# One layer of the second image pair is issued beside the first pair's later layers

## The chip, the cores and the metric

The kernel runs on one core of one Trainium2 chip. The metric is the device time of one execution in microseconds (us). Its engines are named as in the profile: PE (TensorE, matmuls), DVE (VectorE), ACT (ScalarE), POOL (GpSimd) and SP (SyncE, which here only issues DMAs). "Granted clock" is the share of its full speed that TensorE's clock was given in a stretch.

## What is computed

A batch of 8 images of 64 channels and 64 x 64 pixels goes through four layers in turn, all in float32:

```python
# layer 0: full self-attention over the 4096 pixels of an image (bn + relu values), then
#          a depthwise 3x3 conv, a 1x1 conv and a residual
# layer 1: two blocks of 8x8 window attention (the second shifted) with an MLP each
# layer 2: a 3x3 filter made of a spatial and a channel part, then a 1x9 conv and a residual
# layer 3: selective scan over 4 directions with 16 states, then a small multi-scale stage
def step(h, inp):
    u_t, dt_t, B_t, C_t = inp
    h = h * jnp.exp(dt_t[..., None] * A) + dt_t[..., None] * B_t[:, :, None, :] * u_t[..., None]
    return (h, jnp.einsum('bkcn,bkn->bkc', h, C_t))
x = _L0_conv_ref(x, ...)
x = _L1_conv_ref(x, ...)
x = _L2_conv_ref(x, ...)
x = _L3_conv_ref(x, ...)
```

Pixels are only mixed within an image, so different images are independent of each other.

## The kernel before

Two images form a pair: their 2 x 64 channels fill the 128 partitions, and a pair's activation `X` is one 128 x 4096 slab (2 MB). There are four pairs, p = 0 to 3. For each pair there are three kinds of work:

- **front(p)** (L1230): `layer0`, `layer1`, `layer2` and `scan_sources`. It is a Python generator which issues a few instructions and then yields a number, its own estimate of their cost. By these numbers `layer0` costs 702 units, `layer1` 784, `layer2` 286 and `scan_sources` 245, 2016 in all.
- **scans(p)** (L1619): 64 units (2 images x 4 directions x 8 pieces of 512 pixels) of 8 steps each, so 512 steps. A step takes two of the 16 states: `fetch` brings two rows each of B and C from memory, spread over all partitions (L1682), `products` multiplies on POOL (L1687), `step` makes two exponentials on ACT (L1707) and two scans on DVE (L1710), multiplies by C on POOL or, in part, on DVE (L1721 to L1724), and `sums` adds both states up on PE (L1737).
- **back(p)** (L1755): what follows the scan, costed as a quarter of a front.

The order: front(0) runs alone. Then scans(0) runs with front(1) beside it, scans(1) with back(0) and front(2), scans(2) with back(1) and front(3), scans(3) with back(2), and back(3) runs alone. "Beside" is done in the issuing order: after step i of the 512, `scans` draws from the other generators until they have issued the share (i + 1) / (512 - 24) of their total cost. So a step carries 2016 / 488 = 4.13 units of front(1) in scans(0), and the last 24 steps carry none. A scheduler then orders instructions by priority (the order of issue) and readiness.

In `layer0` the main loop runs over 8 column pieces and 32 row tiles: two score matmuls `s` (L1271, one per image), two exponentials `e` (L1277), two value matmuls `po` (L1263), 2.2 units each time. In `layer1`, `window_head` (L1342) and `window_row` (L1383) work on rows of 8 windows: scores `w_s` (L1398), exponentials `w_e` (L1415), values `w_av` (L1425), 37 units a row, 16 rows; `mlp` (L1479) follows twice. `layer2`'s inner loop has nine pairs of a `pb` (L1532) and an `acc` matmul (L1536) per chunk, and `py` (L1546).

Buffers: PSUM is cut into two pools. `ps` holds three rotating banks "da" and one bank "y" (sum of a scan), `pf` three rotating banks "f" and one "acc". The scans draw from `ps`, a front from `pf`. When `turn` is not negative, `bank` (L1179) hands out "f" and "da" in turn, so a front that runs alone has six rotating banks; this is set for front(0). In SBUF there are three slabs in one pool, the scans' buffers (`Y`, 16 KB a partition, and the pool `scan`) stand below them, and each stage opens a small pool of its own (`w0`, `w0b`, `w1n` and so on).

Of the kernel before, what the change touches and what calls it, by code (L numbers as in the profile page):

```python
# [1 line left out]

# [1 line left out]

# [5 lines left out]
F32 = mybir.dt.float32  # L10
# [7 lines left out]
P = 128  # L18
# [6 lines left out]
TD = 512  # L25
NTD = L // TD
LEAD = 24
TC = 1024
NTC = L // TC
SLAB = 66 * 66  # L30
# [195 lines left out]
class _Net:  # L226
    def __init__(self, ctx, tc, x, packs, layout, out):
        self.tc, self.nc = tc, tc.nc
        self.x, self.out = x, out
        nc = self.nc  # L230
        self.const = ctx.enter_context(tc.tile_pool(name="const", bufs=1))
        self.dram = ctx.enter_context(tc.tile_pool(name="rows", bufs=2, space=bass.MemoryType.DRAM))
        self.packs, self.layout, self.w = packs, layout, {}
        self.load(self.const, (0, 1))
        with tc.tile_pool(name="temp", bufs=1) as temp:
            self.load(temp, (2,))
            self.prepare()
# [910 lines left out]
class _Direct:  # L1148
# [8 lines left out]
    def __init__(self, net, ctx):  # L1157
        self.net, self.tc, self.nc, self.w = net, net.tc, net.nc, net.w
        tc = self.tc
        self.dram = ctx.enter_context(tc.tile_pool(name="mem", bufs=2, space=bass.MemoryType.DRAM))  # L1160
        one = ctx.enter_context(tc.tile_pool(name="scan1", bufs=1))
        self.Y = one.tile([P, L], F32, name="Y", tag="Y")
        self.carries = one.tile([P, NST], F32, name="carry", tag="carry")
        self.sw = ctx.enter_context(tc.tile_pool(name="scan", bufs=2))
        self.slabs = ctx.enter_context(tc.tile_pool(name="slabs", bufs=3))
        self.ps = ctx.enter_context(tc.tile_pool(name="ps_scan", bufs=3, space=PSUM))
        self.pf = ctx.enter_context(tc.tile_pool(name="ps_front", bufs=3, space=PSUM))
        self.kept = {}
        self.turn = -1

    def padded(self, name):
        t = self.slabs.tile([P, SLAB], F32, name=name, tag="slab").rearrange("p (h w) -> p h w", w=66)
# [6 lines left out]
    def bank(self, name, shape=(P, CH), ours="f"):  # L1179

        if self.turn >= 0:
            self.turn += 1
            ours = ("f", "da")[self.turn % 2]
        return (self.pf if ours == "f" else self.ps).tile(list(shape), F32, name=name, tag=ours)

    def total(self, name, shape=(P, CH)):
        return self.pf.tile(list(shape), F32, name=name, tag="acc", bufs=1)
# [40 lines left out]


    def front(self, p):  # L1230
        X = yield from self.layer0(p)
        yield from self.layer1(X)
        yield from self.layer2(X)
        yield from self.scan_sources(p, X)

    def layer0(self, p):


        nc, tc, w, net, half = self.nc, self.tc, self.w, self.net, self.HALF
        X = self.flat("X")  # L1240
        nc.sync.dma_start(X, self.net.x[2 * p : 2 * p + 2].rearrange("b c h w -> (b c) (h w)"))
        att = self.padded("att")
        VT = self.flat("VT").rearrange("p (t c) -> p t c", c=P)

        def at(rows, t):
            return X[rows, t * P : (t + 1) * P]

        with tc.tile_pool(name="w0", bufs=2) as wk:
            for g in range(8):
                pv = self.bank("pval", (P, 4, P))  # L1250
                nc.tensor.matmul(pv, lhsT=net.ones[0:1, :], rhs=net.b1row.rearrange("o a c -> o (a c)").unsqueeze(1).to_broadcast([1, 4, P]), start=True, stop=False)
                for j in range(4):
                    nc.tensor.matmul(pv[:, j, :], lhsT=at(slice(0, P), 4 * g + j), rhs=net.w1bd, start=False, stop=(j == 3))
                nc.scalar.activation(VT[:, 4 * g : 4 * g + 4, :], pv, AF.Relu)
                yield 4

            parts = wk.tile([P, 2, 32, NCH], F32, name="parts", tag="parts", bufs=1)
            for jc in range(NCH):
                po = self.total("po")

                def weigh(t, es):
                    for im in range(2):
                        nc.tensor.matmul(  # L1263
                            po[half[im]], lhsT=VT[:, t, half[im]], rhs=es[im], start=(t == 0), stop=(t == 31)
                        )

                last = None
                for t in range(32):
                    ss = [self.bank(f"s{im}") for im in range(2)]
                    for im in range(2):  # L1270
                        nc.tensor.matmul(  # L1271
                            ss[im], lhsT=at(half[im], t), rhs=X[half[im], jc * CH : (jc + 1) * CH], start=True, stop=True
                        )
                    es = []
                    for im in range(2):
                        e = wk.tile([P, CH], F32, name="e", tag="e", bufs=6)
                        nc.scalar.activation(  # L1277
                            e, ss[im], AF.Exp, scale=C**-0.5, accum_out=parts[:, im, t, jc : jc + 1]
                        )
                        es.append(e)  # L1280
                    if last is not None:
                        weigh(*last)
                    last = (t, es)
                    yield 2.2
                weigh(*last)
                nc.vector.tensor_copy(self.rows(att, jc), self.img(po))

            sums = net.sums[:, p]
            nc.vector.tensor_reduce(sums, parts, AX.X, ALU.add)
            rec = wk.tile([P, 2, 32], F32, name="rec", tag="rec", bufs=1)  # L1290
            nc.vector.reciprocal(rec, sums)
            for g in range(8):
                pr = self.bank("prec")
                for j in range(4):
                    for im in range(2):
                        nc.tensor.matmul(
                            pr[half[im], j * P : (j + 1) * P],
                            lhsT=rec[:, im, 4 * g + j : 4 * g + j + 1].to_broadcast([P, 64]),
                            rhs=w["ident"],
                            start=True,  # L1300
                            stop=True,
                        )
                d = self.rows(att, g)
                nc.vector.tensor_tensor(d, d, self.img(pr), ALU.mult)
                yield 4
        with tc.tile_pool(name="w0b", bufs=2) as wk:
            for c in range(NCH):
                acc = self.bank("cacc", (P, 8, 64))
                yield from self.dwconv(acc, att, 8 * c, 8, w["dw2"], None)
                cv = wk.tile([P, 8, 64], F32, name="cv", tag="cv")  # L1310
                nc.scalar.activation(cv, acc, AF.Relu, scale=net.bn23[:, 0:1], bias=net.bn23[:, 1:2])
                pw = self.bank("pw")
                nc.tensor.matmul(pw, lhsT=w["w3bd"], rhs=cv, start=True, stop=True)
                t = wk.tile([P, CH], F32, name="t", tag="t")
                nc.scalar.activation(t, pw, AF.Identity, scale=net.bn23[:, 2:3], bias=net.bn23[:, 3:4])
                x = X[:, c * CH : (c + 1) * CH]
                nc.vector.tensor_tensor(x, x, t, ALU.add)
                yield 3
        return X
# [514 lines left out]
            net.log_exp(last)  # L1834


@with_exitstack
def tile_kernel(ctx: ExitStack, tc: tile.TileContext, x: bass.AP, packs, layout, out: bass.AP):
    net = _Net(ctx, tc, x, packs, layout, out)
    with ExitStack() as path:  # L1840
        net.open(path, True)
        d = _Direct(net, path)
        net.log_exp()
        d.turn = 0
        front = d.run(d.front(0))
        d.turn = -1
        back = 0.25 * front
        for p in range(B // 2):
            works, cost = [], 0
            if p:  # L1850
                works.append(d.back(p - 1))
                cost += back
            if p + 1 < B // 2:
                works.append(d.front(p + 1))
                cost += front
            d.scans(p, d.chain(*works), cost)
        d.run(d.back(B // 2 - 1))

    with tc.tile_pool(name="check", bufs=1) as pool:
        bad = net.in_range(pool)  # L1860
    with tc.If(bad > 0), ExitStack() as path:
        net.open(path, False)
        for p in range(B // 2):
            t = net.layer0(p)
            t = net.layer1(t)
            t = net.layer2(t)
            net.layer3(t, p)
# [21 lines left out]
```

## Time and profile before

| | us |
|---|---|
| median of 3 runs (14009.71 to 14023.95) | 14022.91 |
| the profiled execution | 14012.53 |
| its span, first to last instruction | 14010.7 |
| front(0) alone, until the first product of scans(0) | about 1880 |
| scans(0) with front(1), first to last sum | 1904 to 4915 |
| scans(1) with back(0), front(2) | 4934 to 8257 |
| scans(2) with back(1), front(3) | 8277 to 11611 |
| scans(3) with back(2) | 11632 to 13760 |
| back(3) alone | 13760 to 14010 |

The page's line of 40 slices shows the same in coarse: POOL has nothing to do in the first five slices, which are front(0). Busy shares over the whole span are 81% for PE, 60% for DVE, 50% for ACT and 58% for POOL. They are averages over these stages and say little of any one of them. In scans(3), which has little beside it, POOL is busy for 1819.91 of 2128 us, and a step takes 4.2 us.

The page follows the chain of waits backward from the last instruction over the last stage alone; for the stages that the change touches it has no entry, and the tables by stage are used instead.

### The profile page before, as it was taken

The page shows a single profiled execution, that of the slowest core. Times are in us where ns is not written, and L with a number is a line of the kernel's source. Part 1 is how long each engine was busy: PE and PEld are TensorE (multiplying, and loading weights), DVE is VectorE, ACT ScalarE, POOL GpSimd, SP SyncE. Part 2 cuts the span into 40 slices and gives each one's busy share as a digit, 9 for nine tenths or more (in the row PEclk, how much of TensorE's full clock was granted, in tenths as well). Part 3 has the DMA queues.
Part 4 walks back from the last instruction along what each step waited for, and adds up shares of the span by engine and source line. Part 5 has one row for each costly group of instructions (what it writes and reads, how often), then busy time and mean ns, then how long its engine had stood idle before and what let it go on. Part 6 is the DMA issues. An engine that isn't in the chain of part 4 may idle for free. (4 is left out here: it accounts for less than half of the span.)

```text
span 14010.7 us, 141613 instructions
## 1 busy us (share of the span) xinstructions
PE 11364.2 (81%) x46358; PEld 4240.7 (30%) x46358; DVE 8425.0 (60%) x9763; ACT 7041.2 (50%) x15460; POOL 8178.9 (58%) x4111
## 2 busy tenths in 40 slices
PE   9888979978888669988889667997998866666665
PEld 2255222234433222224433222223443222222221
DVE  0222254477766874356675767337666677997875
ACT  5533156556544645555553645555554554454442
POOL 0000046578767765556665685457666688878982
PEclk9966789989889789998899788998888878888887
DMA  0000044456555754445554675335544577878882
GB/s 17 1 1 2 6 163 162 159 185 226 195 181 189 246 195 149 135 154 176 176 177 160 227 248 172 131 132 189 173 163 166 183 253 259 273 250 275 276 273 97
DMA packets 705499, 2379.23 MB, mean 170 GB/s; under 512 B 81060, under 2 KB 81188, under 8 KB 703980
## 3 DMA queue, kind: packets, MB, share of 16 engines
q1 hardware_dynamic: 681024, 2315.57, 48.9%
q10 hardware_dynamic: 23724, 54.50, 1.0%
q8 instruction: 367, 6.01, 0.2%
q14 instruction: 384, 3.15, 0.1%
HBM read 2269.08 MB, written 100.66 MB: 169 GB/s over the span
## 5 line engine op out<-in xcount | busy, mean ns | idle before, releaser
L1687 POOL TENSOR_TENSOR vd<-B,du 128x1024 f32<-128x1024 f32 x2048 | 4841.8, 2369 | 3920.1 <-DMA B<-rows 2103.0
L1737 PE MATMUL yd<-vd,pack 128*128 128x512 f32 x8192 | 4625.9, 695 | 1265.4 <-POOL vd L1721 449.5
L1710 DVE TENSOR_TENSOR_SCAN hd<-dad,carry,vd 128x512 f32<-128x512 f32 x2464 | 3093.2, 1271 | 1146.2 <-ACT dad L1707 669.9
L1707 ACT ACTIVATE dad<-du,As 128x512 f32<-128x512 f32 x4096 | 2718.4, 680 | 1017.3 <-DVE hd L1710 701.9
L1737 PEld LDWEIGHTS yd<-vd,pack 128*128 128x128 f32 x8192 | 1624.1, 215 | 3956.6 <-issue 1863.1
L1721 POOL TENSOR_TENSOR vd<-hd,C 128x1024 f32<-128x1024 f32 x768 | 1811.7, 2359 | 1324.0 <-DVE hd L1710 695.7
L1723 POOL TENSOR_TENSOR vd<-hd,C 128x512 f32<-128x512 f32 x1280 | 1637.0, 1280 | 317.9 <-DVE hd L1710 230.0
L1277 ACT ACTIVATE e<-s 128x512 f32<-128x512 f32 x2048 | 1199.2, 591 | 1030.1 <-PE s L1271 1028.6
L1710 DVE TENSOR_TENSOR_SCAN dad<-dad,carry,vd 128x512 f32<-128x512 f32 x1120 | 1427.6, 1275 | 126.5 <-POOL vd L1687 77.5
L1271 PE MATMUL s<-X 64*128 64x512 f32 x4096 | 1343.5, 647 | 105.5 <-ACT e L1277 105.3
L1263 PE MATMUL po<-e,VT 128*64 128x512 f32 x4096 | 1155.4, 631 | 19.0 <-ACT e L1277 19.0
L1718 ACT ACTIVATE carry<-hd 128x1 f32<-128x1 f32 (+1 forms) x1792 | 357.3, 201 | 1225.9 <-DVE hd L1710 1215.5
L1724 DVE TENSOR_TENSOR vd<-dad,C 128x512 f32<-128x512 f32 x1280 | 860.9, 673 | 72.7 <-ACT carry L1718 62.4
L1425 PEld LDWEIGHTS w_av<-vals,w_e 64*64 64x64 f32 x16384 | 630.9, 163 | 204.5 <-ACT w_e L1415 99.4
L1425 PE MATMUL w_av<-vals,w_e 64*64 64x9 f32 x16384 | 658.6, 218 | 38.2 <-ACT w_e L1415 38.0
L1271 PEld LDWEIGHTS s<-X 64*128 64x128 f32 x4096 | 363.5, 187 | 1052.4 <-issue 823.7
L1710 DVE TENSOR_TENSOR_SCAN hd<-dad,vd 128x512 f32<-128x512 f32 x352 | 420.1, 1211 | 191.7 <-ACT dad L1707 88.3
L1748 DVE TENSOR_TENSOR Y<-Y,yd 128x512 f32<-128x512 f32 x128 | 124.8, 975 | 661.3 <-PE yd L1737 661.1
L1718 ACT ACTIVATE carry<-dad 128x1 f32<-128x1 f32 x1120 | 189.5, 169 | 616.6 <-DVE dad L1710 614.4
L1415 ACT ACTIVATE w_e<-w_e 128x512 f32<-128x512 f32 x512 | 310.8, 627 | 360.7 <-DVE w_e L1410 239.4
L1410 DVE TENSOR_TENSOR w_e<-w_s,bias 128x512 f32<-128x512 f32 x512 | 328.8, 682 | 236.3 <-PE w_s L1398 235.3
L1263 PEld LDWEIGHTS po<-e,VT 128*64 128x64 f32 x4096 | 212.9, 136 | 824.6 <-issue 581.0
(247 smaller groups left out, 11150.5 us busy)
## 6 DMA issues: line engine op xcount, KB each, us to landing
B<-rows SPq DMA_DIRECT2D x2048, 512.0 KB, 5.0
C<-rows SPq DMA_DIRECT2D x2048, 512.0 KB, 4.5
xs<-xt SPq DMA_DIRECT2D x128, 256.0 KB, 2.9
xs<-xc SPq DMA_DIRECT2D x128, 256.0 KB, 3.4
xc<-xcv ACTq DMA_DIRECT2D x64, 256.0 KB, 3.8
zs<-z ACTq DMA_DIRECT2D x64, 256.0 KB, 3.8
xt<-XT ACTq DMA_DIRECT2D x32, 512.0 KB, 7.8
rows<-bc SPq DMA_DIRECT2D x256, 64.0 KB, 2.0
```

The lines of the kernel that those rows point to most:

```text
L1263: nc.tensor.matmul(po[half[im]], lhsT=VT[:, t, half[im]], rhs=es[im], start=(t == 0), stop=(t == 31))
L1271: nc.tensor.matmul(ss[im], lhsT=at(half[im], t), rhs=X[half[im], jc * CH : (jc + 1) * CH], start=True, stop=True)
L1277: nc.scalar.activation(e, ss[im], AF.Exp, scale=C**-0.5, accum_out=parts[:, im, t, jc : jc + 1])
L1425: nc.tensor.matmul(self.av[half[im], x % 4 + j, h, :], lhsT=es[h // 4][half[im], j, h % 4, :], rhs=V[half[im], x + j, h, :], start=True, s ...
L1687: self.nc.gpsimd.tensor_tensor(v, st["B"], dx.to_broadcast([P, 2, TD]), ALU.mult)
L1707: nc.scalar.activation(da, u["du"][:, 0], AF.Exp, scale=net.As[:, k, n : n + 1])
L1710: nc.vector.tensor_tensor_scan(along(to), along(da), along(v[:, j]), first, ALU.mult, ALU.add)
L1718: nc.scalar.activation(cs, ends, AF.Copy)
L1721: st["w"] = nc.gpsimd.tensor_tensor(v, h, CC, ALU.mult)
L1723: st["w"] = nc.gpsimd.tensor_tensor(v[:, 0], h[:, 0], CC[:, 0], ALU.mult)
L1724: nc.vector.tensor_tensor(v[:, 1], hs[1], CC[:, 1], ALU.mult)
L1737: m = nc.tensor.matmul(y, lhsT=w["ident"], rhs=st["v"][:, j], start=(n == 0), stop=(n == NST - 1))
```

## The change

`layer0` of pair 1 is taken out of scans(0). It is issued in a new method `begin`, beside `layer1`, `layer2` and `scan_sources` of pair 0, in that order of issue: after `layer0` of pair 0 is done (front now yields a 0 there), it draws 0.8 units of the other generator for each unit of front(0). With 702 units to issue it is through after 702 / 0.8 = 877 units of front(0), that is after all of `layer1` (784) and the first 93 units of `layer2`. Its three slabs and one working pool lie where `Y` and the scans' pool are opened afterwards. Its result goes to memory (2 MB) and front(1) starts by loading it, in the place of the load of the input. Its PSUM is the pool `ps`, three banks "da" and the bank "y". `turn` stays negative in front(0), which therefore has the three banks "f" instead of six, in its own `layer0` too. In scans(0), the cost beside is 1315 units instead of 2016.

```diff
+AHEAD = 0.8
...
+    def begin(self, ctx):
...
+        with tc.tile_pool(name="slabs0", bufs=3) as slabs, tc.tile_pool(name="w00", bufs=2) as pool:
+            ahead = _Apart(self, slabs, pool).first(1)
+            front = first = done = 0
+            for cost in self.front(0):
+                front += cost
+                if cost == 0:
+                    first = front
+                while first and done < AHEAD * (front - first):
+                    done += next(ahead, front)
+            self.run(ahead)
+        one = ctx.enter_context(tc.tile_pool(name="scan1", bufs=1))
+        self.Y = one.tile([P, L], F32, name="Y", tag="Y")
+        self.carries = one.tile([P, NST], F32, name="carry", tag="carry")
+        self.sw = ctx.enter_context(tc.tile_pool(name="scan", bufs=2))
+        return front, first
...
     def front(self, p):
-        X = yield from self.layer0(p)
+        if ("first", p) in self.kept:
+            X = self.flat("X")
+            self.nc.sync.dma_start(X, self.kept["first", p])
+        else:
+            X = yield from self.layer0(p)
+        yield 0
...
+class _Apart(_Direct):
...
+    def bank(self, name, shape=(P, CH)):
+        return self.ps.tile(list(shape), F32, name=name, tag="da")
+
+    def total(self, name, shape=(P, CH)):
+        return self.ps.tile(list(shape), F32, name=name, tag="y", bufs=1)
...
+    def first(self, p):
+        X = yield from self.layer0(p)
+        kept = self.kept["first", p] = self.memory("first")
+        self.nc.sync.dma_start(kept, X)
...
-        d.turn = 0
-        front = d.run(d.front(0))
-        d.turn = -1
+        front, first = d.begin(path)
...
-                cost += front
+                cost += front if p else front - first
```

More of the change, by code (lines that the diff above doesn't have):

```diff
@@ L1 @@
-from contextlib import ExitStack
+from contextlib import ExitStack, nullcontext
 import numpy as np
@@ L1160, in __init__ @@
         self.dram = ctx.enter_context(tc.tile_pool(name="mem", bufs=2, space=bass.MemoryType.DRAM))
[L1161 to L1164, printed above, removed]
         self.slabs = ctx.enter_context(tc.tile_pool(name="slabs", bufs=3))
@@ L1169, in __init__, with work @@
         self.turn = -1
+    def begin(self, ctx):
+        tc = self.tc
+        with tc.tile_pool(name="slabs0", bufs=3) as slabs, tc.tile_pool(name="w00", bufs=2) as pool:
[13 more added lines that the diff above has]
+        return front, first
+    def work(self, name):
+        return self.tc.tile_pool(name=name, bufs=2)
     def padded(self, name):
@@ L1246, in at @@
             return X[rows, t * P : (t + 1) * P]
-        with tc.tile_pool(name="w0", bufs=2) as wk:
+        with self.work("w0") as wk:
             for g in range(8):
@@ L1305, in layer0 @@
                 yield 4
-        with tc.tile_pool(name="w0b", bufs=2) as wk:
+        with self.work("w0b") as wk:
             for c in range(NCH):
@@ L1834, in back, with __init__, work @@
             net.log_exp(last)
+class _Apart(_Direct):
+    def __init__(self, d, slabs, pool):
+        self.net, self.tc, self.nc, self.w = d.net, d.tc, d.nc, d.w
+        self.ps, self.slabs, self.pool, self.dram, self.kept = d.ps, slabs, pool, d.dram, d.kept
+    def bank(self, name, shape=(P, CH)):
+        return self.ps.tile(list(shape), F32, name=name, tag="da")
+    def total(self, name, shape=(P, CH)):
+        return self.ps.tile(list(shape), F32, name=name, tag="y", bufs=1)
+    def work(self, name):
+        return nullcontext(self.pool)
+    def first(self, p):
+        X = yield from self.layer0(p)
+        kept = self.kept["first", p] = self.memory("first")
+        self.nc.sync.dma_start(kept, X)
 @with_exitstack
```

## The prediction

> **What bounds the kernel now.** I read the line of slices first, then cut the span at the stages' borders (first and last sum of each scan, first and last matmul of each layer) and asked for the busy table of these stretches, then for the PE's timeline inside them, and last for who waited for whom. The table of stretches (us; per engine busy time and count; granted clock; DMA share; GB/s):
>
> ```profile
> 62.00:592.00 530.00, 530.00 (x2028) 129.54 (x2024) 4.85 (x7) 320.41 (x1016) 0.00 (x0) 1.00 0.00 1
> 648.00:1502.00 854.00, 717.05 (x6392) 395.35 (x6390) 225.70 (x447) 311.17 (x465) 0.00 (x0) 0.66 0.01 2
> 1904.00:2872.00 968.00, 928.25 (x2698) 257.42 (x2698) 429.64 (x404) 565.21 (x1591) 595.55 (x290) 0.98 0.49 165
> 3090.00:3448.00 358.00, 329.74 (x3282) 172.73 (x3281) 263.85 (x341) 204.22 (x407) 277.21 (x136) 0.91 0.64 213
> 4068.00:4527.00 459.00, 418.12 (x833) 152.20 (x832) 292.53 (x336) 174.99 (x371) 298.93 (x147) 0.92 0.52 175
> 1904.00:4915.00 3011.00, 2606.91 (x11328) 972.14 (x11326) 1940.84 (x2182) 1672.44 (x3698) 2096.44 (x1018) 0.91 0.57 192
> 8215.00:8252.00 37.00, 21.28 (x35) 7.49 (x36) 26.61 (x26) 12.68 (x22) 37.00 (x19) 0.87 0.72 254
> ```
>
> Line 1 is the main loop of layer0 for pair 0: PE without a gap at full clock, 530 us for 256 tiles, 2.07 us a tile. Line 2 is front(0) from the end of layer0 to 93 units into layer2, exactly what the change puts beside the other layer0: PE looks 84% busy, but at a clock of 0.66, the other engines are mostly idle. Lines 3 to 5 are scans(0) beside layer0, the first window attention and layer2 of pair 1; PE is busy for 96, 92 and 91%. Line 6 is scans(0) whole. Line 7 shows scan steps with nothing beside them: POOL has no gap, at two steps in 8.27 us on its timeline, 4.14 us a step. What a busy PE is worth at either clock is seen in two timelines, of layer2 alone (clock 0.50 there) and of window attention inside scans(0):
>
> ```profile
> 1419.23 2.07 PE L1532 MATMUL pb<-f,pack 18*128 18x512 f32 x2
> 1421.23 2.08 PE L1536 MATMUL acc<-tap,pack 128*128 128x512 f32 x2
> ...
> 3130.78 1.02 PE L1662 MATMUL pdd<-xs,xdt 128*128 128x512 f32 x2
> 3131.63 1.02 PE L1359 MATMUL w_q<-w_h,pack 128*128 128x512 f32 x2
> 3189.96 1.98 PE L1737 MATMUL yd<-vd,pack 128*128 128x512 f32 x4
> 3195.37 2.04 PE L1425 MATMUL w_av<-vals,w_e 64*64 64x9 f32 x64
> ```
>
> A float32 matmul of 512 columns is two records: 2.0 us a pair at half clock, about 0.96 from start to start at full clock. That POOL, in scans(0), waits for the PE more than for anything else is in the waits of POOL over 1904 to 4915:
>
> ```profile
> POOL vd L1687 <- PE yd L1737: 303.2, 107, 12.5
> POOL vd L1721 <- issue: 182.6, 40, 9.7
> POOL vd L1721 <- DVE hd L1710: 180.5, 63, 10.4
> ```
>
> **What the skill says.** "TensorE: Matmul & The Clock Gate", What's actually happening: the matrix clock stands at half unless recent activity releases it, and only the two shares 4/8 and 8/8 occur. This trace agrees: the stretches' 0.66 is a mean of 0.50 and 1.00, and the pairs above take 2.0 against 0.96 us. "Perfetto Trace Analysis", Identifying the Most-Contended Engine: matmul busy time is a bad measure of the distance to the engine's limit. Here line 2 says so: 84% busy, at two thirds of the clock. "PSUM — Partial Sum Buffer", Specifications: eight banks a partition, which is why the second stream needs the scans' four, and front(0) loses three.
>
> **The change, part by part.** I count PE work as full-clock demand, from start-to-start times at clock 1.00.
>
> 1. Layer0 of one pair: main loop 530 us; eight `pval` groups at about 2 us, 16; `prec` 8 and eight `pw` 8. Sum 562 us. The convolution's DVE work (72 operations of 0.74 us, 54 us in all) can lie beside PE.
>
> 2. What stands in 648 to 1502: a window row is 4 x 1.02 (`w_s`, 16 records) + 4 x 1.97 (`w_av`, 64 records) + 1.1 + 0.96 + 0.93 + 0.95 (`pc`, `pv`, `w_q`, `w_k`) + 1.08 (`w_vv`) + 0.9 (`w_ot`) + 1.0 (`w_pp`) = 18.9 us; 16 rows 302. First norm 8 x 1.82 = 15. Two MLPs, 16 x 3.9 = 62. Layer2 chunks at 2 x 0.96 + 9 x 2.0 + 7.9 = 27.8, 2.45 of them (85 units of 34.7 after the eight copies): 68. Sum 447 us, which took 854: half of the stretch is a slow clock and waits.
>
> 3. Together 1009 us of demand. PE doesn't run at 100% of demand where streams are mixed. Scans(0) and scans(1) show how far it gets: a step's own demand is 1.91 (`yd`) + 1.94 / 8 (`pdd`, `pbc`) = 2.15 us. Beside layer0: 256 tiles in 143 steps, 1.79 x 2.07 + 2.15 = 5.86 against 6.76 us measured, 87%. Beside window attention (0.51 us a unit): 296 units in 68 steps, 4.37 against 5.27, 83%; in scans(1) 296 in 47.5, 5.33 against 6.81, 78%. Beside layer2: 0.78 a unit, 5.1 against 6.12, 84%. I take 84%, since dense layer0 tiles are 56% of the mix: 1009 / 0.84 = 1201 us. Against 854 the opening grows by **+347**. Bounds: 92% gives 1097 (+243), 74% gives 1363 (+509).
>
> ACT would be busy 311 + 256 x 1.58 (exponential and its accumulator read, two each) + 20 = 735 of 1201 us and DVE under 300: neither becomes the bound. Behind a waiting PE or ACT instruction the other stream's work is queued too: a row's `window_head` makes PE wait for square, logarithm, exponential and a DVE product. PE's waits in 650 to 1500 sum to about 140 us, the longest kinds being:
>
> ```profile
> PE w_q L1359 <- DVE w_h L1355: 36.9, 16, 2.3
> PE ph L1490 <- DVE m_h L1486: 36.2, 16, 2.5
> ```
>
> Layer0's tiles are independent of these and fill part; the rest is in the 84%.
>
> 4. Scans(0) loses layer0: 1315 units over 488 steps, 2.69 a step instead of 4.13. PE demand falls to 2.15 + about 0.6 x 2.69 = 3.8 us a step, which at 83% is 4.6; POOL needs 2096 / 512 = 4.1; DVE (1941 less some 80 of layer0's: its convolution, copies and adds) / 512 = 3.6. So three engines come near each other, and what is late next is POOL, then the chain through DVE. By stage: window attention cost 5.27 us a step at 4.35 units and 6.81 at 6.23, 0.82 us a unit, so the line would pass under POOL's floor; I take 4.7 for 220 steps. Layer2: 6.12 at 3.81 and 7.37 at 5.02, so 5.0 at 2.69; 4.9 for 106 steps. The MLP took 5.3 us at both densities, so something other than PE holds it; 5.0 for 71 steps with the norm. Sources 5.8 and 6.4; 4.9 for 91. Sum 1033 + 519 + 355 + 446 = 2353, and 24 steps without company at 4.15 add 100: 2453 against 3011, **-558**. Bounds: 4.4 a step (2247, -764) and 5.2 (2638, -373).
>
> 5. Small parts. Three banks instead of six for layer0 of pair 0: the same loop has three inside scans(0), and its tiles start 2.06 us apart there (2200.86, 2202.92), so I price it at +10 for the handovers and layer2's rest, bounds 0 and +50. The load of `X` for front(1) was there before (one SP DMA, issued at 1862.56) and is as large; the store of 2 MB is issued on SP at about two thirds of front(0), where DMA is 1% busy, with only the stores of `x2` behind it. At the 190 to 290 GB/s seen in scans it takes some 7 to 11 us, hidden; uncovered it would cost those 11. The input's load for pair 1 has its own slab and lands during layer0 of pair 0. The scans' buffers wait for slabs that are free 300 us earlier.
>
> Sum: 347 - 558 + 10 = **-201**. On the profiled execution 14012.5 gives 13,812; the median of the runs shown stands 10 above it, so 13,822 us.
>
> **Rivals.** (a) *Larger gain*: layer0 keeps the clock at 1.00 and fills every gap, 92%, and scans(0) gets to 4.4 us a step: 243 - 764 + 10 = -511, 13,512. For it: beside layer0 the clock is 0.98. Against: no mixed stretch exceeds 87%, and a POOL-bound 4.4 occurs only where PE is little used.
> (b) *Conserved*: PE sets both stretches and work is just moved; 80% gives +407, scans(0) at 5.1 gives -422: -5, 14,018. For it: the MLP's 5.3. Against: POOL's waits for PE vanish and half the opening's clock is unused.
> (c) *Slower*: the gate doesn't open. Window attention's 64-row tiles leave the clock at 0.66 when alone; if interleaved layer0 runs at that too, its 562 us take 851 beside the 717 already busy, 1568: +714. With -558 and +10 that is +166, 14,189. It decides from the point where the joint stretch is longer than 1402 us (72% of demand). For it: 78% was seen in scans(1). Against: clock 0.91 in attention beside `yd`, whose share of the demand was lower (49%) than layer0's here.
> That the streams don't overlap at all would be 854 + 562 / 0.97, +579, nearly (b).
>
> **Numbers.** Chances: forecast 0.62, (a) 0.13, (b) 0.10, (c) 0.15. A measurement of this kernel tells about 0.2% (28 us) from nothing. Faster: 0.62 + 0.13 + a little of (b), 0.77; within 0.2%: most of (b), 0.08; slower 0.15. Range: the forecast's bounds combined (not both ends at once) reach from about -380 to +10; (a) and (c) leave their outer halves out: 13,640 to 14,050.
>
> **What would show it.** Right: the joint stretch from 648 lasts near 1200 us with PE over 90% busy and a clock above 0.85; first sum of scans(0) near 2260; its sums span near 2450 us at about 4.8 us a step, with POOL's wait for `yd` well under 303 us. Wrong: a clock under 0.75 in the joint stretch (c), or steps above 5.2 us with little on PE, which would mean that a chain or the rows' DMA, not PE, sets scans(0). Scans(1) to (3) should keep 3323, 3334 and 2128 us.

## The result: 13791 us, and where the time went

| | before | changed |
|---|---|---|
| median, us (4 runs each) | 14016.31 | 13791.44 |
| lowest to highest | 13987.48 to 14023.95 | 13790.06 to 13842.86 |
| ratio, 95% interval | | 0.9847, 0.9828 to 0.9867 |

The changed kernel is 225 us faster by the medians. The profiled execution took 13842.86 us, the longest of its four, so the two profiles differ by 170 us only; the stages below are those of the profiles. First the table of stretches of the changed kernel (us; per engine busy time and count; granted clock; DMA share; GB/s):

```profile
62.00:600.00 538.00, 538.00 (x2033) 132.24 (x2032) 4.85 (x7) 322.52 (x1017) 0.00 (x0) 1.00 0.00 1
648.00:1840.00 1192.00, 1162.67 (x8581) 453.61 (x8580) 320.31 (x586) 637.70 (x1486) 0.00 (x0) 0.94 0.01 4
1840.00:2190.00 350.00, 246.56 (x374) 77.94 (x372) 145.06 (x222) 84.78 (x121) 0.00 (x0) 0.68 0.10 37
2222.00:4720.00 2498.00, 2004.36 (x9112) 811.69 (x9110) 1860.46 (x2078) 1372.21 (x2664) 2092.46 (x1021) 0.88 0.68 232
2257.00:2821.00 564.00, 467.34 (x3514) 215.75 (x3512) 415.48 (x479) 298.99 (x614) 485.81 (x238) 0.90 0.67 231
```

Line 1 is the main loop of layer0 for pair 0, as before. Line 2 is the joint stretch, from 648 until layer0 of pair 1 is done: 1192 us where 854 stood, PE busy for 98% at a clock of 0.94. (It reaches a little further into layer2: 57 of its 144 `acc` records have begun at 1840, against 42 at 1502 before. Further down, stretches are compared at the same record.) Line 3 is what is left of front(0), at the old 0.68. The first sum of scans(0) comes at 2222 instead of 1904, so the opening grew by 318 us. Line 4 is scans(0): 2498 us against 3011, 513 less. Line 5 is its first window attention, 118 steps at 4.78 us. The rest of the kernel holds 3337, 3344 and 2124 us for scans(1) to (3), against 3323, 3334 and 2128. And the waits of POOL within scans(0), a list that had begun with 303 us for PE:

```profile
POOL vd L1746 <- issue: 123.0, 36, 10.0
POOL vd L1746 <- DVE hd L1735: 81.7, 35, 9.8
POOL vd L1712 <- DMA B<-rows: 60.7, 42, 6.6
POOL vd L1712 <- PE yd L1762: 39.3, 22, 8.0
```

The wait for PE fell to 39 us. So the time moved the way the sum had it: -513 in scans(0), +318 in the opening. What needed testing was why.

### The profile page after: what moved, and what is told of

It is laid out like the page before. It is cut to its first block, busy times and chain, and to the rows that moved or that the text cites. A ratio compares the mean times of both kernels' runs of the same rounds, so it can differ in the third digit from the quotient of the medians.

```text
span 13841.1 us, 141364 instructions
## 1 busy us (share of the span) xinstructions
PE 11209.6 (81%) x46358; PEld 4137.2 (30%) x46358; DVE 8419.5 (61%) x9763; ACT 7076.0 (51%) x15475; POOL 8170.1 (59%) x4111
## 5 line engine op out<-in xcount | busy, mean ns | idle before, releaser
L1288 PE MATMUL po<-e,VT 128*64 128x512 f32 x4096 | 1197.7, 628 | 13.3 <-ACT e L1302 13.2
L1450 PEld LDWEIGHTS w_av<-vals,w_e 64*64 64x64 f32 x16384 | 561.0, 147 | 196.4 <-issue 87.9
L1450 PE MATMUL w_av<-vals,w_e 64*64 64x9 f32 x16384 | 589.3, 208 | 25.5 <-ACT w_e L1440 25.4
L1687 PE MATMUL pdd<-xs,xdt 128*128 128x512 f32 x512 | 338.7, 749 | 185.1 <-DVE hd L1735 72.4
```

The costliest lines, as they stand in the source:

```text
L1288: nc.tensor.matmul(po[half[im]], lhsT=VT[:, t, half[im]], rhs=es[im], start=(t == 0), stop=(t == 31))
L1450: nc.tensor.matmul(self.av[half[im], x % 4 + j, h, :], lhsT=es[h // 4][half[im], j, h % 4, :], rhs=V[half[im], x + j, h, :], start=True, s ...
```

## The experiments

Each ran beside runs of the kernel before on the same chip; its median there was 14015 to 14028 us.

**The changed kernel again**, unaltered.

> The changed kernel again, unaltered, for a second profile: its profiled execution took 13842.86 us while three others took 13790 to 13793. If that execution was only the slowest of its kind, this one shows a span near 13789 us, the joint stretch from 648 near 1192 us, the sums of scans(0) over 2498 us, and scans(1) and scans(2) at 3323 to 3334 us as before the change.

Median 13795.58 us, ratio 0.9836 (0.982 to 0.9853). Its profiled execution was again the longest of its four, 13831.61. The joint stretch was 1192 us to the microsecond and scans(0) 2483. Scans(1) and (2) were 3342 and 3346, again some 15 us above before. In the other experiments, whose code for them is the same, they lie anywhere from 3320 to 3350, so I take this as scatter between executions. Another part of the excess lies in the opening, as the section on split pairs shows; why these profiled executions are the long ones stays open.

**Layer0 of pair 1 after front(0).** Its load is held back by a wait on the last activation of `scan_sources`:

```diff
-AHEAD = 0.8
+AHEAD = 0.0
...
+            apart.after = self.silu
             self.run(ahead)
...
+        if self.after is not None:
+            tc.add_manual_dep(load.ins, self.after.ins.name, ...Sync..., reason="after the front")
```

> Layer0 of pair 1 waits until the whole front(0) is done, then runs alone; scans(0) is as in the changed kernel. Theory (the gain of the change comes from lying beside layer1, whose clock and waits left half of PE unused): the opening grows by about 562 us plus 54 us of convolution over that of before instead of 317, so this kernel takes 13791 + 300 = about 14090 us, slower than before. Rival (the gain is that scans(0) sheds its overload, whatever the opening does): within 60 us of the changed kernel.

Measured 14203.75 us, 408 more than the changed kernel, 114 more than the theory had, and slower than before: ratio 1.0131 (1.0112 to 1.015). Its stretches are the rest of front(0), layer0 alone, and scans(0):

```profile
648.00:1934.00 1286.00, 1001.85 (x6816) 473.16 (x6816) 382.15 (x691) 402.74 (x592) 0.00 (x0) 0.65 0.03 10
1934.00:2615.00 681.00, 604.11 (x2292) 163.51 (x2291) 77.49 (x109) 359.13 (x1081) 8.60 (x4) 0.92 0.06 22
2615.00:5085.00 2470.00, 1983.94 (x9115) 804.79 (x9114) 1860.67 (x2080) 1373.65 (x2667) 2090.21 (x1021) 0.89 0.70 234
```

Scans(0) gains as much as in the changed kernel (2470 us). One after the other the two parts take 1967 us, side by side 1574 (648 to 2222): 393 us come from lying beside each other. Without that the change loses. Alone, layer0 costs 681 us rather than the 616 of the expectation: PE waits 13 us for its load, the convolution takes 63 us instead of 54, and 31 us pass from its end to the first sum, for the store, the loads and the first step.

**Three banks alone.** The kernel before, without its six banks in front(0):

```diff
-        d.turn = 0
         front = d.run(d.front(0))
-        d.turn = -1
```

> The kernel before with one part of the change: front(0) has three rotating banks instead of six, and nothing else. Theory (layer0's tiles need no more than three): 0 to +10 us against before. Rival (the banks cost the change a part of its gain): +20 to +50 us.

Measured 14080.15 us, 1.0046 (1.003 to 1.0061), 52 us slower: the theory is out, and the loss has the size that the rival named, though in the kernel before. The main loop of layer0 is as fast, its convolution takes 75 us instead of 65. But look at the first MLP, before and with three banks:

```profile
971.00:1039.00 68.00, 47.15 (x101) 12.07 (x101) 12.01 (x16) 44.91 (x56) 0.00 (x0) 0.80 0.00 0
```

```profile
980.00:1070.00 90.00, 60.07 (x101) 15.87 (x99) 12.02 (x16) 44.66 (x55) 0.00 (x0) 0.65 0.00 0
```

The same instructions take 90 instead of 68 us, and 93 instead of 61 in the second MLP: 54 us. Window attention and layer2 lose nothing and are some 17 us shorter together, so the opening as a whole grows by 42 us in the profiles. Why an MLP needs the banks was not looked into.

**Filler beside front(0).** Is it the gap or the clock that layer0 fills? The kernel before, with three banks and full-array matmuls of no use:

```diff
+            if front > 702:
+                due += cost
+            while due >= 4:
+                due -= 4
+                t = d.ps.tile([P, CH], F32, name="fill", tag="da")
+                net.nc.tensor.matmul(t, lhsT=net.w["ident"], rhs=net.w["w2bd"][:, 0:4, :].rearrange(...), start=True, stop=True)
```

> The kernel before with three banks in front(0), and beside layer1, layer2 and the sources of pair 0 one full-array matmul of 512 columns per 4 units, 329 of them, into a bank that nobody reads: 0.96 us each at full clock, 316 us of demand. It adds work that the result does not need. Theory (dense neighbours open the clock gate for layer1): the stretch from 648 to the end of the first 93 units of layer2 takes 780 to 860 us although 210 us of demand are added to its 854, at a clock above 0.8; the kernel stays within +60 us of before. Rival (the clock stays at 0.66 there and only gaps are filled): the stretch takes 1000 us or more, the kernel +200 us or more.

Measured 14035.88 us, 1.0007 (1.0001 to 1.0014): 8 us above before, and 44 below its own base, the kernel with three banks. The stretch from 648 to the end of layer1, first with three banks, then with the filler too, and last with the filler up to the 42nd `acc` record, which is where 1502 lies in the kernel before:

```profile
648.00:1445.00 797.00, 616.25 (x6260) 343.71 (x6260) 211.16 (x418) 303.70 (x448) 0.00 (x0) 0.64 0.00 1
```

```profile
648.00:1395.00 747.00, 717.51 (x6841) 384.78 (x6840) 219.15 (x430) 303.79 (x450) 0.00 (x0) 0.91 0.01 1
648.00:1501.00 853.00, 814.52 (x6976) 412.94 (x6974) 242.16 (x470) 315.48 (x469) 0.00 (x0) 0.88 0.01 2
```

About 580 more records (290 of the 329 matmuls, some 280 us of demand at full clock; they depend on nothing and moved forward) and the stretch is 50 us shorter, at a clock of 0.91 instead of 0.64. The expectation's stretch, the last line, is 853 us, within the theory's 780 to 860. Work added to PE made PE's other work faster: filling gaps alone could not do that, a faster clock can. That is the gate: layer1 alone leaves it half shut.

**No order, and a wider order.** Layer0 issued last without a wait, and a pace of 0.55:

```diff
-AHEAD = 0.8
+AHEAD = 0.0
```

> Layer0 of pair 1 is issued after the whole of front(0), without a wait, so that the scheduler may still pull it into gaps (in the changed kernel it had pulled the first matmuls of it to 27 us). Theory (the order of issue decides how much lies beside layer1): most of it runs after front(0), 13950 to 14090 us. Rival (the scheduler fills every gap by readiness, and the pace of 0.8 matters little): within 40 us of the changed kernel's 13791, or below it, as front(0) is then never delayed.

13842.08 us, 0.9865 (0.9848 to 0.9881): some 46 to 51 us above the changed kernel, just outside the rival's range and far from the theory's. The scheduler pulls ready work forward by itself; the pace is worth about an eighth of the 408 us that the serial kernel lost.

```diff
-AHEAD = 0.8
+AHEAD = 0.55
```

> Pace 0.55 instead of 0.8: layer0 of pair 1 lies beside all of layer1, layer2 and the sources instead of the first 877 of 1315 units. After 1840 us the changed kernel's front(0) runs alone, PE 246 of 350 us busy at a clock of 0.68. Theory (any stretch of front(0) without dense company wastes clock): the opening shortens by 60 to 120 us, the kernel takes 13670 to 13730 us. Rival (the sources are held by DVE and the end of layer0 with its store and load now comes last): within 30 us of 13791.

13813.75 us, 0.9844 (0.9827 to 0.986), no gain, as the rival had it. Its reason is taken up again below.

**Split pairs.** The joint stretch has 1009 us of counted demand, PE is busy throughout, and between 1000 and 1400 us the clock is 1.00. So what takes 1192? PE's timeline of the changed kernel shows it (start, duration, records):

```profile
1017.34 1.08 PE L1288 MATMUL po<-e,VT 128*64 128x512 f32 x4
...
1034.05 1.07 PE L1288 MATMUL po<-e,VT 128*64 128x512 f32 x2
1035.06 1.13 PE L1230 MATMUL pv<-n_sq,pack 128*128 128x512 f32 x2
1036.12 1.07 PE L1288 MATMUL po<-e,VT 128*64 128x512 f32 x2
```

Each image's `po` uses half of the array. Both together (4 records) take 1.08 us; with an instruction of the other stream between them, each half takes as long by itself. The Trainium skill, "TensorE: Matmul & The Clock Gate", Part 3: Packing small matmuls, says that small matmuls at different positions in the array run concurrently. The trace agrees for halves that are next to each other, and shows that it ends where something stands between them. In the opening 98 halves of `po` and 38 of `s` stand alone, so 68 pairs are split. The edit keeps the halves adjacent: the first waits until the operand of the second is there too, and the second is given priority (likewise for `s`, whose first half waits for an exponential of the tile before):

```diff
+                    m = nc.tensor.matmul(po[half[0]], lhsT=VT[:, t, half[0]], rhs=es[0], ...)
+                    self.gate(m, exps[1])
+                    with tc.high_priority(offset=200):
+                        m1 = nc.tensor.matmul(po[half[1]], lhsT=VT[:, t, half[1]], rhs=es[1], ...)
+                    net.behind(m1, m)
```

> The two half-array matmuls of a layer0 tile (one per image) are kept next to each other on PE, by order and priority alone. In the changed kernel's joint stretch 49 po pairs and 19 s pairs are split by an instruction of the other stream, and a split half takes 1.0 us where the pair side by side takes 1.03. Theory (split pairs are what keeps the joint stretch at 85% of the demand that I counted, as its clock there is 1.00): 50 to 90 us faster than the changed kernel. Rival (the missing 15% are clock and handovers): within 20 us of it.

Measured 13755.71 us, 0.9812 (0.9795 to 0.9829): about 38 us below the changed kernel's medians, between the two expectations. A pair in it, whose halves start together:

```profile
1034.41 0.59 PE L1290 MATMUL po<-e,VT 128*64 128x512 f32 x1
1034.41 0.59 PE L1293 MATMUL po<-e,VT 128*64 128x512 f32 x1
```

Now 24 halves of `po` and 6 of `s` stand alone, 15 pairs instead of 68. The joint stretch up to the same record, the 54th `acc` of layer2: in the changed kernel, in the kernel of the next experiment (whose opening has the same code and as many split pairs), and with the pairs kept:

```profile
648.00:1824.00 1176.00, 1147.37 (x8550) 447.74 (x8548) 312.59 (x574) 633.00 (x1479) 0.00 (x0) 0.94 0.01 2
```

```profile
648.00:1802.00 1154.00, 1125.49 (x8554) 437.50 (x8550) 313.37 (x575) 632.90 (x1481) 0.00 (x0) 0.96 0.01 2
```

```profile
648.00:1759.00 1111.00, 1078.12 (x8572) 424.04 (x8570) 318.65 (x582) 633.21 (x1491) 0.00 (x0) 0.95 0.01 2
```

The first two differ by 22 us and by 0.02 in the clock, with nothing in the code to tell them apart: that much is scatter, and part of why the changed kernel's profiled executions were its longest. Against them the pairs are worth 65 and 43 us; the medians say 38. An estimate from the counts, 53 split pairs fewer at about 1 us each, lies in that range.

**POOL after, POOL before.** Half of the multiplications by C of pair 0 go to DVE instead of a quarter, in the changed kernel and in the kernel before (ACT gets some small copies more with it):

```diff
-        n0, rp = 2 * (i % 8), i % 2 or u["image"] >= B - 2
+        n0, rp = 2 * (i % 8), i % 2 or u["image"] >= B - 2 or u["image"] < 2
```

> In the scans of pair 0 half of the multiplications by C go from POOL to DVE, as scans(3) has it: POOL 3.6 instead of 4.1 us a step, DVE about 3.9 instead of 3.6. Theory (after the change POOL is the nearest bound of scans(0), 2092 of 2498 us busy): its sums take 2350 to 2440 us. Rival (PE with its clock, or the chain through DVE, sets the step of 4.88 us): 2480 us or more.

Measured 13667.18 us, 0.9744 (0.9728 to 0.9761), some 125 below the changed kernel. Scans(0):

```profile
2202.00:4566.00 2364.00, 1990.63 (x9108) 791.85 (x9107) 1989.42 (x2330) 1382.31 (x2875) 1818.77 (x1019) 0.90 0.74 245
```

A step takes 4.62 us, POOL is busy for 77% and DVE and PE for 84% each; POOL's longest wait is now one for the scans on DVE:

```profile
POOL vd L1748 <- DVE hd L1735: 301.4, 194, 7.4
POOL vd L1712 <- DMA B<-rows: 112.6, 70, 6.1
```

> The kernel before with the same shift from POOL to DVE in the scans of pair 0. Theory (before the change PE bound scans(0), and POOL waited for it): at most 40 us faster than before, scans(0) 2970 us or more, where the same shift takes 120 us off the changed kernel. Rival (POOL or its chain held the scans before as well): 100 us faster or more.

Measured 13961.14 us, 0.9965 (0.9951 to 0.9978), 54 less, where the theory allowed 40, with 2944 us in scans(0) instead of 2970 or more: both its bounds are missed by a little. Its scans(0), beside layer0 and after it, and then the second of these in the kernel before (its first is 968 us, shown in the prediction):

```profile
1913.00:2885.00 972.00, 936.06 (x2710) 259.94 (x2708) 470.92 (x477) 570.86 (x1656) 521.99 (x290) 0.97 0.48 164
2885.00:4857.00 1972.00, 1669.77 (x8618) 689.34 (x8614) 1589.08 (x1960) 1119.73 (x2262) 1304.26 (x729) 0.89 0.63 212
```

```profile
2872.00:4915.00 2043.00, 1678.65 (x8634) 714.72 (x8630) 1511.20 (x1779) 1107.24 (x2107) 1500.89 (x729) 0.88 0.61 205
```

Beside layer0 a lighter POOL changes nothing (972 against 968 us), as it must where PE is the bound. Beside the later layers POOL's load cost 71 us even before: POOL had a part in these steps already.

**Both, and the pace again.** The two edits together, at 0.8, 0.65 and 0.55:

> The changed kernel with both alterations that helped: layer0's pairs kept together (-36 us by itself) and half of the multiplications by C of pair 0 on DVE (-124 us by itself). They lie in different stages. Theory (the opening is bound by PE and scans(0) by POOL, each by itself): the gains add, 13620 to 13650 us. Rival (a scan that starts earlier or an opening that ends otherwise takes one of them back): 13660 us or more.

> The same at a pace of 0.65 instead of 0.8. Pace 0.55 gave nothing by itself, but split more pairs. Theory (with the pairs kept, spreading layer0 over all of layer2 fills the slow clock there): 20 to 50 us faster than at 0.8. Rival (the sources are held by DVE, and what is filled in layer2 is lost in layer1): within 15 us.

> Both alterations at the pace of 0.55, which by itself (pairs not kept) gained nothing: it split more pairs, 133 po halves stand alone in its order on PE against 99 in the changed kernel; here 37 do. Theory (the splits took back what the wider spread gained): at least 40 us faster than both alterations at 0.8, 13540 to 13585 us. Rival (at 0.55 the end of layer0, its store and its load come last and hold the opening): 13600 us or more, although 0.65 gave 13558.

At 0.8: 13623.85 us, 0.9723 (0.9709 to 0.9736), so the gains add. At 0.65: 13558.31, 0.9681 (0.9665 to 0.9698), 66 us under 0.8 and more than the 20 to 50 expected. At 0.55: 13590.92, 0.9695 (0.9676 to 0.9714), 33 us under 0.8, just short of the expected 40.

So the wider spread gains once pairs stay together: at 0.55 the step from 0.8 was worth +20 us with the pairs left alone and -33 with them kept. The counts fit that swing. With the pairs left alone, 132 halves of `po` and 113 of `s` stand alone at 0.55, which is 54 split pairs more than at 0.8, at about 1 us each.

That 0.55 isn't better than 0.65 (the runs of the two overlap) fits the traces too. From the last `acc` of layer2 to the first sum, at 0.65 and at 0.55:

```profile
1870.00:2075.00 205.00, 97.78 (x146) 30.02 (x146) 125.18 (x194) 91.95 (x139) 10.15 (x6) 0.64 0.28 107
```

```profile
1848.00:2109.00 261.00, 138.18 (x345) 45.62 (x345) 175.58 (x269) 111.29 (x178) 11.72 (x6) 0.64 0.23 86
```

At 0.55 layer2 ends 22 us earlier, and 56 us are lost behind it: the convolution of layer0 now lies beside that of the sources, both on DVE, and PE waits 71 us there for what follows the former (`pw` for `cv`). That agrees with the reason of the rival at 0.55, though no run takes it apart. Of 0.65, the joint stretch and what is left after it:

```profile
648.00:1893.00 1245.00, 1217.47 (x8875) 474.07 (x8872) 363.35 (x654) 655.95 (x1524) 0.00 (x0) 0.97 0.01 3
1893.00:2040.00 147.00, 58.58 (x78) 17.66 (x76) 101.34 (x154) 57.35 (x79) 0.00 (x0) 0.57 0.24 91
```

Layer0's main loop now ends at 1720, within layer2, and its convolution where the sources begin. The version at 0.65 beats both kernels of this case.

## Why the prediction was right, step by step

| step | predicted | measured |
|---|---|---|
| joint part of the opening (term 3) | +347 | +298 up to the same record of layer2 |
| three banks and the rest of the opening (term 5) | +10 | +20 after that record; +52 for the banks in the kernel before |
| opening, to the first sum | +357 | +318 |
| scans(0) (term 4) | 2453 us, -558 | 2498 and 2483 us, -513 and -528 |
| total | -201, 13822 us | -225, 13791 us |

*The mechanism* held. The opening had PE time and clock to spare, which the serial and the filler kernels show from both sides; and scans(0) was past its PE bound beside layer0, which the shift from POOL to DVE in the kernel before shows. Rival (c), a gate that stays shut, needed 0.66 in the joint stretch; it is 0.94. Rival (b) needed scans(0) at 5.1 us a step; it is 4.88, and rival (a) needed 4.4. The total is closer than its terms: the opening came cheaper than forecast and scans(0) dearer, and that the two cancel is luck.

*Term 3* was somewhat too dear, and its reason was half of the truth. The piece of front(0) from 648 to the 54th `acc`, in the kernel before, to set beside the 1176 us shown above:

```profile
648.00:1526.00 878.00, 741.05 (x6416) 400.98 (x6414) 229.44 (x452) 311.85 (x466) 0.00 (x0) 0.66 0.01 2
```

The demand up to there is about 1021 us (the 1009, and 12 for what layer2 has done beyond 1502), so PE reached 87% of it where 84% was taken. An estimate of where the missing 155 us went: a clock of 0.94 over 1176 us loses about 70, PE sat idle for 29, and 68 split pairs at about 1 us each make 68. Clock and waits were in the forecast's 84%; the split pairs were not, since 2.07 us a tile assumes that two halves stay together, which holds while layer0 runs alone and not under a scheduler that mixes two streams. And the clock was not lost evenly: layer0's main loop ends at 1652, before the first `acc` of layer2 at 1718, so from 1650 to 1840 only its convolution lies beside layer2, at a clock of 0.74. At the pace of 0.65 the main loop reaches into layer2.

*Term 4* was some 30 to 45 us too favourable. Window attention and the first MLP came at 4.7 to 4.9 us a step, near what was taken (4.7 and 5.0); the second MLP took about 5.2 us for its 29 steps (5.0 was taken) and layer2 and the sources 5.1 (4.9 taken). "POOL is late next" holds: taking work from it gave 119 to 134 us in scans(0), although it was busy for only 84% there.

*Term 5* looked for the cost of the banks in the wrong loop. Layer0's main loop has none, as argued; in the kernel before, the MLPs lose 54 us when front(0) runs alone. What they lose in the changed kernel, where layer0's tiles lie between, wasn't tried, as the second stream holds the other banks there. One loss can be seen in it: from the last `acc` of layer2 to the first sum, where nothing lies beside the sources, it takes 202 us against 183. The last convolution of the sources ends 159 us after that `acc` instead of 142, and with three banks in the kernel before after 169, so the banks are the likely reason.

*The full serial case* was priced at +579 for the opening. Measured were 711 (2615 against 1904). Front(0) by itself ends 61 us later there (1940 against 1879), and layer0 adds 649: 572 for its parts on PE, 63 for its convolution, for which the price had nothing, and the rest for load and start.

*Two readings* of the lines were a little off. The two steps of POOL in 8215 to 8252 repeat after 8.14 us, not 8.27, so 4.07 us a step; over the 24 steps without company that is 2 us. And full-array matmuls of 512 columns start 0.85 to 0.97 us apart at full clock (3130.78, 3131.63), where 0.96 was taken for all.

## What to carry to other kernels

Before moving work beside other work, convert the busy time of PE into demand at full clock: here an engine that showed 84% had half of its time to give, and company even sped up what was there. Then check that the mixing leaves pairs of half-array matmuls next to each other, since a scheduler that orders by readiness can split them. Compare stretches at the same instruction of the same work, not at round marks, and ask what two executions of the same code differ by before a gain of that size is explained. When a stage loses its bound, name the next engine in line and lighten it in the same step: here that was worth more than half as much as the change itself.

## What was not expected of the hardware

- Useless matmuls made a stretch shorter: 797 to 747 us with 290 added, the clock going from 0.64 to 0.91.
- A PE without a gap can stand at half clock: in layer2 the clock was 0.50 with PE busy for 20 of 20 us (1420 to 1440 in the kernel before), where a `pb` with its 18-row operand and a full `acc` take turns, about 2.0 us each. The operand alone doesn't decide it: where three `pb` follow each other behind the 18 records of `py` (1536 in the same trace), their six records took 2.84 us, which is full clock. What does decide it, no run here shows.
- A half-array matmul of 512 columns costs as much alone (1.07 us) as the pair side by side (1.08 us), so one instruction between the two halves costs a microsecond beyond its own time.
- Of the stages of front(0), the MLPs needed rotating PSUM banks most: three instead of six made an MLP 22 to 32 us longer and the clock of the first fall from 0.80 to 0.65, while layer0's dense main loop lost nothing.
- The same program, with as many split pairs, ran its joint stretch in 1154 and in 1176 us, at clocks of 0.96 and 0.94.
